# Self-attention in two-slot steps: order of transposes, outputs and small copies

## Chip, cores and metric

The kernel runs on one NeuronCore of a Trainium2 chip. The metric is the device time in microseconds of one execution, launch to end. The engines are named as in the profile: PE (TensorE, with PEld for its weight loads), DVE (VectorE), ACT (ScalarE), POOL (GpSimd) and SP (SyncE, which issues the transfers).

## What is computed

A decoder block on x (8 x 224 x 512, float32) with a context (8 x 750 x 384). Three layers follow one another, each with a residual sum and a layernorm behind it:

```
x = layernorm(x + self_attention(x))     # 16 heads of 64
x = layernorm(x + cross_attention(x, context))
x = layernorm(x + ffn(x))                # ternary weights, 8-bit activations

def self_attention(t):
    t = t * rsqrt(mean(t*t) + eps) * norm_w
    q, k, v = t @ Wq, t @ Wk, t @ Wv     # split into 16 heads
    q = q / |q| * (q_gamma + 1) * 8      # norm over each head's 64 numbers
    k = k / |k| * (k_gamma + 1) * 8
    s = tanh(q k^T / 50) * 50 / 8
    return softmax(s) v @ Wo
```

Only the self-attention is touched by the change.

## The kernel before

The 1792 rows of x lie in 14 tiles of 128 rows. Self-attention works on four groups `g` of two batch elements (448 columns). Inside a group it goes through eight pairs of heads `hp`, so the main loop has 32 slots, `m = 8 g + hp`. Two slots, an even and an odd one, belong together: in the even slot m the generator `project_pair` computes q and k of the slots m+2 and m+3 together, by a scheme with seven half-size products in place of eight (`mm_x`, `mz` as `mm_z`), and it is advanced piece by piece with `next(pair)` between other work. Instructions are issued on each compute engine in the order in which this Python code emits them (`manual_schedule`). Only the transfers on SP are ordered by a planner.

What a slot does, with names and lines of the kernel before:

- `self_scores(m)` (L490): PE makes the scores (`sc_a`, L500), ACT applies tanh (L510) and exp (L516) into `pr`.
- `inverse_sums(m)` (L520), a generator: DVE sums `pr` over blocks of 32 by a transposing reduction (L526, `sm_q`), three copies on ACT gather the partitions (L536), DVE adds and inverts (L539, L544, `sm_i`), three copies on ACT spread the result over partitions (L550), and DVE transposes it into `rc_a` (L558). It is advanced with `next(sums)`, in part in the following slot.
- `self_values(m - 1)` (L564): PE multiplies the previous slot's `pr` with the values (`ov_a`, L572), DVE scales into `oT` (L580). In groups 0 and 2 POOL copies 64 columns of `oT` into `oT_tail` (L585), since an output tile straddles two groups.
- `head_norms(m + 2, ...)` (L424), a generator used in even slots: DVE reduces the squares of q and k (L430, `nm_q`), four copies on ACT bring the neighbour quarter (L440, `nm_o`), and POOL adds, clamps and takes the power -1/2 for the two slots (L444, L445, L129 `nm_i`). This last part is emitted in the odd slot.
- `scale_qk(m)` (L455): DVE transposes `nm_i` (L458) and scales q and k with it (L463). The scores of slot m need this.
- `project_v` (L468): PE computes values of one tile (`mm_v`, L474), ACT copies them out (`copy_v`, L486).
- For the next group: `square` and `rms_norms` (ACT L245, DVE L249, POOL L129 `rms_rs`) when `hp == 0`, `scale_x` (ACT L256, `xn`) for one tile a slot, `transpose_xn` (PE L264, `tr_x`) and `copy_xn` (DVE L268, `xnT`) a slot later, for `hp` 1 to 3 or 4. `sum_input` (POOL L360 to L364) and `sum_weights` (POOL or DVE, L327 to L330) prepare operands of the seven products.
- `self_output` (L587): PE multiplies a finished tile of the previous group with Wo (`mm_o`, L600), DVE adds it to x (L609). The list `out_at` says in which `hp` of each group that happens. The tile is then put on `due`; in the next slot `layernorm` takes its statistics (DVE L136 to L138), its root on POOL (L129 `ln_rs`), and at the end of the slot DVE scales x (L152).

Some loops of the self-attention share PSUM buffers: `mm_x`, `mm_z`, `mm_v`, `tr_x` and `mm_o` take turns in three (`a_mm`).

Of the kernel before, what the change touches and what calls it, by code (L numbers as in the profile page):

```python
# [20 lines left out]
F32 = mybir.dt.float32  # L21
BF16 = mybir.dt.bfloat16
# [11 lines left out]
B, S, DIM = 8, 224, 512  # L34
# [4 lines left out]
P = 128  # L39
# [6 lines left out]
NPAIR = HEADS // 2  # L46
# [16 lines left out]
def decoder_block(ctx: ExitStack, tc: tile.TileContext, a: dict, out: bass.AP):  # L63
    nc = tc.nc
# [75 lines left out]
    def layernorm(tiles):  # L140


        n = len(tiles)
        mv = stat.tile([P, n, 2], F32, tag=f"ln_mv{n}", name="ln_mv")
        ve = stat.tile([P, n, 1], F32, tag=f"ln_ve{n}", name="ln_ve")
        rs = stat.tile([P, n, 1], F32, tag=f"ln_rs{n}", name="ln_rs")
        for j, i in enumerate(tiles):
            statistics(x[i], mv[:, j, :], ve[:, j, :])
        rsqrt(rs[:, :, 0], ve[:, :, 0])
        def scale():  # L150
            for j, i in enumerate(tiles):
                nc.vector.tensor_scalar(  # L152
                    x[i], x[i], mv[:, j, 0:1], rs[:, j, :], ALU.subtract, ALU.mult
                )

        return scale
# [54 lines left out]
    TAIL = G % P  # L211
# [5 lines left out]
    with tc.tile_pool(name="a_sb", bufs=2) as sb, tc.tile_pool(  # L217
        name="a_mm", bufs=3, space=PSUM
    ) as ps_mm, tc.tile_pool(name="a_sc", bufs=2, space=PSUM) as ps_sc, tc.tile_pool(
        name="a_ov", bufs=1, space=PSUM  # L220
# [20 lines left out]
            nc.gpsimd.memset(pr[KEYS[1][1] :, :, 1], 0.0)  # L241

        def square(i):
            sq = sb.tile([P, DIM], F32, name="sq_x", bufs=1)
            nc.scalar.activation(sq, x[i], AF.Square, accum_out=rms[:, i : i + 1])  # L245

        def rms_norms(i0, i1):
# [12 lines left out]
        def transpose_xn(i):  # L260
            y = xn.pop(i)
            trs[i] = tr = ps_mm.tile([P, KD, P], F32, tag="mm", name="tr_x")
            for k in range(KD):
                nc.tensor.transpose(tr[:, k, :], y[:, k * P : (k + 1) * P], ident)  # L264

        def copy_xn(i):
            c = i * P % (2 * G)
            nc.vector.tensor_tensor(  # L268
                xnT[:, :, c : c + P], trs.pop(i), norm_w.to_broadcast([P, KD, P]),
                ALU.mult,  # L270
            )
# [152 lines left out]
        def head_norms(m, i0, i1):  # L424

            quarter = sb.tile([P, 2, 4 * NB], F32, name="nm_q")[:, i0:i1]
            quarter = quarter.rearrange("p n b -> p (n b)")
            nc.vector.tensor_reduce(  # L430
                quarter,
                sq_pair[:, i0:i1].rearrange("p n u w (b c) -> p (n u w b) c", c=Q32),
                AX.X, ALU.add, apply_transpose=True,
            )
            yield
            other = sb.tile([P, 2, 4 * NB], F32, name="nm_o", bufs=1)[:, i0:i1]
            other = other.rearrange("p n b -> p (n b)")
            for q in range(P // Q32):
                o = q ^ 1
                nc.scalar.copy(  # L440
                    other[q * Q32 : (q + 1) * Q32], quarter[o * Q32 : (o + 1) * Q32]
                )
            yield
            nc.gpsimd.tensor_tensor(quarter, quarter, other, ALU.add)  # L444
            nc.gpsimd.tensor_scalar(quarter, quarter, 1e-24, None, ALU.max)  # L445
            for i in range(i0, i1):
                inv[m + i] = sb.tile([P, 2, 2 * NB, 1], F32, name="nm_i")
                at = (i - i0) * 4 * NB
                rsqrt(
                    inv[m + i].rearrange("p u b o -> p (u b o)"),  # L450
                    quarter[:, at : at + 4 * NB],
                )
            yield
# [66 lines left out]
        def inverse_sums(m):  # L520

            quarter = sb.tile([P, 2, 2, NB, NT, P // Q32], F32, name="sm_q", bufs=1)
            for u in range(2):
                nc.vector.tensor_reduce(  # L526
                    quarter[:, u, :, :, :, 0].rearrange("p j b t -> p j t b"),
                    prs[u].rearrange("p j t (b c) -> p j t b c", c=Q32),
                    AX.X, ALU.add, apply_transpose=True,
                )  # L530
            yield


            flat = quarter.rearrange("p u j b t g -> p (u j b t) g")
            for g in range(1, P // Q32):
                nc.scalar.copy(flat[:Q32, :, g], flat[g * Q32 : (g + 1) * Q32, :, 0])  # L536
            yield
            tot = sb.tile([Q32, 2, 2, NB], F32, name="sm_t", bufs=1)
            nc.vector.tensor_reduce(  # L539
                tot.rearrange("p u j b -> p (u j b)"),  # L540
                quarter[:Q32].rearrange("p u j b t g -> p (u j b) (t g)"), AX.X, ALU.add,
            )
            isum = sb.tile([P, 2, 2 * NB, 1], F32, name="sm_i", bufs=1)
            nc.vector.reciprocal(  # L544
                isum[:Q32, :, :, 0].rearrange("p j (u b) -> p j u b", u=2),
                tot.rearrange("p u j b -> p j u b"),
            )
            yield
            for g in range(1, P // Q32):
                nc.scalar.copy(  # L550
                    isum[g * Q32 : (g + 1) * Q32, g // 2, :, 0],
                    isum[:Q32, g // 2, :, 0],
                )
            yield
            rcs[m] = sb.tile([P, 2, S], F32, name="rc_a", bufs=1)
            for j in range(2):
                half = slice(j * DH, (j + 1) * DH)
                nc.vector.transpose(  # L558
                    rcs[m][half].rearrange("p u q -> p (u q)"),
                    isum[half, j].to_broadcast([DH, 2 * NB, Q32]),  # L560
                )
            yield

        def self_values(m):  # L564
            g, hp = divmod(m, NPAIR)
            ov = ps_ov.tile([P, 2, 256], F32, name="ov_a")
            for u in range(2):
                vt, pr = v[2 * g + u, hp // 4], prs[u]
                for kt, (_, n) in enumerate(KEYS):
                    for j in range(2):  # L570
                        h0, c = j * DH, (2 * hp + j) % 8 * DH
                        nc.tensor.matmul(  # L572
                            ov[h0 : h0 + DH, u, :S],
                            lhsT=vt[:n, kt, c : c + DH],
                            rhs=pr[:n, j, kt, :],
                            start=(kt == 0),
                            stop=(kt == NT - 1),
                        )
            oT[m] = sb.tile([P, 2, S], F32, name="oT", bufs=15)
            nc.vector.tensor_tensor(oT[m], ov[:, :, :S], rcs.pop(m), ALU.mult)  # L580
            if g % 2 == 0:

                if hp == 0:
                    tails[g] = sb.tile([P, NPAIR, TAIL], F32, name="oT_tail", bufs=1)
                nc.gpsimd.tensor_copy(tails[g][:, hp, :], oT[m][:, 1, S - TAIL :])  # L585

        def self_output(g, i, hp0=0, hp1=NPAIR):  # L587
# [24 lines left out]
        tails, outs, due, scales = {}, {}, [], []  # L612
# [35 lines left out]
        for i in opened[0][2:]:  # L648
            project_v(i, 0)()

        out_at = [(), (1, 3, 5), (1, 3, 5, 6), (5, 6, 7)]
        nothing = iter(lambda: None, 0)
        sums = norms = nothing
        for m in range(NS):
# [9 lines left out]
            if even:  # L664
                next(pair)
                next(sums)
                if m > 0:
                    scale_qk(m)
                next(pair)
                next(sums)  # L670
                next(pair)
                next(sums)
                next(pair)
            next(sums)
            if m > 0:
                self_values(m - 1)
            next(norms)
            next(pair)
            self_scores(m)
            for i in due:  # L680
                scales.append(layernorm([i]))
            due.clear()
            if even:
                scale_qk(m + 1)
            next(pair)
            if turned is not None:
                transpose_xn(turned)
                if not even:
                    copy_xn(turned)
            copy_v = lambda: None  # L690

            if hp % 4 < len(tiles):
                copy_v = project_v(tiles[hp % 4], c)
            if not even:
                copy_v()
            sums = inverse_sums(m)
            next(sums)
            norms = nothing
            if even:
                if pair is not nothing:  # L700
                    norms = head_norms(m + 2, 0, 2)
                next(norms)
                next(sums)
                copy_v()
                next(norms)
                next(sums)
                next(sums)
                if turned is not None:
                    copy_xn(turned)
            for f in scales:  # L710
                f()
            scales.clear()
# [700 lines left out]
```

## Time and profile before

| | us |
|---|---|
| median of 3 runs (lowest to highest) | 1728.12 (1725.98 to 1728.61) |
| the profiled execution | 1727.02 |
| its span, first to last instruction | 1725.2 |
| busy in the span: PE, PEld | 1671.9, 1148.8 |
| busy in the span: DVE, ACT, POOL | 1210.7, 938.7, 671.7 |

The page gives busy time per engine over the whole span. A row of the timeline has the start in us, the duration in us of the instructions merged into it, the engine, the line of the kernel, the operation with the tile written and the tiles read, and how many instructions there are; brackets hold the idle time of the engine before it and what ended that. A line of a windows table has the stretch, its length, the busy us (and instructions) of PE, PEld, DVE, ACT and POOL, the granted PE clock, the DMA share and the GB/s. A row of groups ends in busy us and mean ns of one, and the idle time before.

### The profile page before, as it was taken

The numbers are of one execution on the slowest core, as the hardware profiler recorded it, in microseconds if no ns is written. First come the engines' busy times: TensorE is split into PE (matmuls) and PEld (weight loads), VectorE is DVE, ScalarE is ACT, GpSimd is POOL, SyncE is SP. The second block draws the span as 40 slices with busy tenths as digits, with TensorE's granted clock in tenths as the row PEclk, the third lists the DMA queues.
The fourth block names the chain that finished last, engine by engine and source line by source line (L and its number), as shares of the span: only waits on it lengthen the run. The fifth ranks groups of instructions, "written<-read, shape, count | busy, mean of one in ns | idle before, by whom it ended". The sixth has DMA issues, their size and how long they took to land.

```text
span 1725.2 us, 24169 instructions
## 1 busy us (share of the span) xinstructions
PE 1671.9 (97%) x8962; PEld 1148.8 (67%) x8962; DVE 1210.7 (70%) x2402; ACT 938.7 (54%) x1752; POOL 671.7 (39%) x577
## 2 busy tenths in 40 slices
PE   8898999998999999999999999999999999999998
PEld 5666566566654777777676777777776776774443
DVE  3576566555773777677787787797875776886877
ACT  4677647555750566555565565464443543445663
POOL 3562342352430343444344244344343343443244
PEclk9999999999999999999999999999999999999999
DMA  7043112111312122111112112000000000031434
GB/s 256 25 137 126 43 55 74 43 51 48 123 64 90 63 74 101 50 50 64 43 48 84 44 50 82 22 34 34 1 3 29 4 5 24 1 129 40 74 81 106
DMA packets 85572, 106.71 MB, mean 62 GB/s; under 512 B 38352, under 2 KB 58832, under 8 KB 82512
## 3 DMA queue, kind: packets, MB, share of 16 engines
q1 hardware_dynamic: 85456, 105.19, 19.2%
q8 instruction: 70, 1.15, 0.3%
q14 instruction: 46, 0.38, 0.1%
HBM read 82.36 MB, written 14.16 MB: 56 GB/s over the span
## 4 chain that ended last, share of the span: by engine, by line
PE 87%; DVE 5%; ACT 3%; POOL 2%; issue 1%; DMA 1%; SPq 0%; POOLq 0%; DVEq 0%; ACTq 0%
PE mm_k L948 15%; PE mm_v L936 14%; PE sc_c L985 9%; PE ov_c L1079 9%; PE mm_co L194 6%; PE mm_q L961 6%; PE mm_f L1214 5%; PE mm_o L600 5%; PE mm_v L474 4%; PE mm_x L382 4%; PE mm_z L382 3%; PE dn L1302 2%; PE sc_a L500 2%; PE ov_a L572 2%; POOL nm_i L129 1%
## 5 line engine op out<-in xcount | busy, mean ns | idle before, releaser
L1069 POOL TENSOR_TENSOR csh<-cpT 125x672 f32<-125x672 f32 x128 | 207.3, 1620 | 579.7 <-DVE cpT L1059 553.5
L1067 ACT ACTIVATE cpT<-cpT 125x1344 f32<-125x1344 f32 x128 | 169.7, 1326 | 227.9 <-DVE cpT L1059 218.7
L948 PE MATMUL mm_k<-cT,xattn_Wk 128*128 128x375 f32 x768 | 259.4, 487 | 1.6 <-DMA cT<-ctxT 1.6
L936 PE MATMUL mm_v<-xattn_Wv,cT 128*125 128x256 f32 x1152 | 259.1, 379 | 0.0
L936 PEld LDWEIGHTS mm_v<-xattn_Wv,cT 128*125 128x125 f32 x1152 | 216.3, 188 | 28.8
L993 ACT COPY cpT<-sc_c 125x448 f32<-125x448 f32 x384 | 173.8, 560 | 108.2 <-PE sc_c L985 106.0
L948 PEld LDWEIGHTS mm_k<-cT,xattn_Wk 128*128 128x128 f32 x768 | 140.4, 189 | 102.1 <-issue 13.1
L1059 DVE TENSOR_TENSOR cpT<-cpT,mx_b 125x1344 f32<-125x1344 f32 x128 | 193.2, 1550 | 2.2
L995 DVE TENSOR_TENSOR cm<-sc_c,cpT 125x448 f32<-125x448 f32 x128 | 74.0, 619 | 147.4 <-ACT cpT L993 147.4
L985 PE MATMUL sc_c<-cqT,ckT 64*125 64x224 f32 x1536 | 163.5, 359 | 3.0 <-DVE cqT L969 3.0
L1079 PE MATMUL ov_c<-cpT,cv 125*64 125x224 f32 x1536 | 159.4, 357 | 0.0
L985 PEld LDWEIGHTS sc_c<-cqT,ckT 64*125 64x125 f32 x1536 | 140.8, 185 | 27.4 <-ACT ckT L955 14.3
L129 POOL TENSOR_TENSOR nm_i<-nm_q,mhalf 128x28 f32<-128x28 f32 x32 | 153.4, 4807 | 1.4
L1079 PEld LDWEIGHTS ov_c<-cpT,cv 125*64 125x64 f32 x1536 | 104.6, 137 | 47.3 <-issue 17.9
L955 ACT COPY ckT<-mm_k 128x375 f32<-128x375 f32 x128 | 59.2, 462 | 127.3 <-PE mm_k L948 127.3
L961 PEld LDWEIGHTS mm_q<-xT,xattn_Wq 128*128 128x128 f32 x512 | 96.8, 190 | 16.2
L474 PE MATMUL mm_v<-wv,xnT 128*128 128x512 f32 x224 | 107.5, 627 | 0.0
L961 PE MATMUL mm_q<-xT,xattn_Wq 128*128 128x224 f32 x512 | 107.2, 352 | 0.0
L600 PE MATMUL mm_o<-attn_Wo,oT 128*128 128x512 f32 (+1 forms) x224 | 100.0, 601 | 0.0
L1214 PE MATMUL mm_f<-ternary,xqT 128*128 128x512 bf16 x448 | 98.7, 379 | 0.9 <-DVE x L1106 0.9
L194 PE MATMUL mm_co<-xattn_Wo,coT 128*128 128x512 f32 (+1 forms) x256 | 98.1, 594 | 0.0
L1070 POOL TENSOR_TENSOR csm<-csh 125x224 f32<-125x224 f32 x128 | 93.8, 732 | 10.0
(187 smaller groups left out, 2643.5 us busy)
## 6 DMA issues: line engine op xcount, KB each, us to landing
w_pair<-w_sums_all SPq DMA_DIRECT2D x24, 512.0 KB, 4.1
cT<-ctxT SPq DMA_DIRECT2D x8, 1125.0 KB, 5.7
w_stage<-w_gateT SPq DMA_DIRECT2D x8, 1024.0 KB, 5.2
w_stage<-w_upT SPq DMA_DIRECT2D x8, 1024.0 KB, 5.1
w_stage<-w_downT SPq DMA_DIRECT2D x8, 1024.0 KB, 5.2
tern<-w_t SPq DMA_DIRECT2D x24, 256.0 KB, 2.3
ternary<-tern SPq DMA_DIRECT2D x3, 2048.0 KB, 12.6
w_pair<-attn_Wq SPq DMA_DIRECT2D x36, 128.0 KB, 2.2
```

Of the source, the lines that this page charges most:

```text
L194: nc.tensor.matmul(mm[row : row + m, :], lhsT=oT[:, k, at : at + m], rhs=w[:, k, :], start=(k == 0), stop=(k == NPAIR - 1),)
L474: nc.tensor.matmul(mm, lhsT=xnT[:, k, at : at + P], rhs=wv[:, k, c * 512 : (c + 1) * 512], start=(k == 0), stop=(k == KD - 1),)
L600: nc.tensor.matmul(mm[row : row + lhsT.shape[-1], :], lhsT=lhsT, rhs=wo[:, hp, :], start=(hp == 0), stop=(hp == NPAIR - 1),)
L936: nc.tensor.matmul(mm[:, i, :], lhsT=cT[:, k, c * CT : (c + 1) * CT], rhs=xwv[:, k, g * VN : (g + 1) * VN], start=(k == 0), stop=(k == KC ...
L948: nc.tensor.matmul(mm, lhsT=xwk[:, k, hp * P : (hp + 1) * P], rhs=cT[:, k, c * HALF : (c + 1) * HALF], start=(k == 0), stop=(k == KC - 1),)
L961: nc.tensor.matmul(mm, lhsT=xwq[:, k, hp * P : (hp + 1) * P], rhs=xT[:, k, :], start=(k == 0), stop=(k == KD - 1),)
L985: nc.tensor.matmul(sc[j][:, i, :], lhsT=kT[h0 : h0 + DH, ct * CT : (ct + 1) * CT], rhs=qT[h0 : h0 + DH, :], start=True, stop=True,)
L993: nc.scalar.copy(pT[:, j, 2 * c2 : 2 * c2 + 2, :], sc[j])
L1059: nc.vector.tensor_tensor(pT[:, j], pT[:, j], nm[:CT, j] .rearrange("p (o q) -> p o q", o=1) .to_broadcast([CT, NCT, S]), ALU.add,)
L1069: nc.gpsimd.tensor_tensor(half, pT[:, j, 0:3], pT[:, j, 3:6], ALU.add)
L1079: nc.tensor.matmul(ov[h0 : h0 + DH, :], lhsT=v[:, ct, hq * DH : (hq + 1) * DH], rhs=pT[:, j, ct, :], start=(ct == 0), stop=(ct == NCT - 1),)
L1214: nc.tensor.matmul(mm, lhsT=xqTs[i][:, k, :], rhs=w[:, k, cols], start=(k == 0), stop=(k == KD - 1),)
```

## The change

- In a slot that has both, the transposes `transpose_xn` are emitted behind the value projection instead of ahead of it; in odd slots `copy_v` comes before `copy_xn`.
- The statistics and the root of `layernorm` for the tiles on `due` are emitted right behind `self_values`, ahead of the norm roots, where they stood behind `self_scores`.
- In group 2 the output of `hp = 6` moves to `hp = 7`, so that all outputs but the last group's `hp = 6` lie in odd slots.
- `oT_tail` gets the pool's two buffers instead of one.
- The four copies of L440 and the three of L550 go from ACT to DVE. The three of L536 stay on ACT. In a pair of slots that is 10 of 16 small copies.
- The generators lose the yields around these copies: in a slot's second half the copies, the sums and the transposes into `rc_a` are emitted together, in the following slot.
- The squares that `square` writes and nobody reads become bfloat16.

```diff
         def square(i):
-            sq = sb.tile([P, DIM], F32, name="sq_x", bufs=1)
+            sq = sb.tile([P, DIM], BF16, name="sq_x", bufs=1)
...
                 AX.X, ALU.add, apply_transpose=True,
             )
-            yield
             other = sb.tile([P, 2, 4 * NB], F32, name="nm_o", bufs=1)[:, i0:i1]
             other = other.rearrange("p n b -> p (n b)")
             for q in range(P // Q32):
                 o = q ^ 1
-                nc.scalar.copy(
+                nc.vector.tensor_copy(
                     other[q * Q32 : (q + 1) * Q32], quarter[o * Q32 : (o + 1) * Q32]
                 )
             yield
...
-            yield
             for g in range(1, P // Q32):
-                nc.scalar.copy(
+                nc.vector.tensor_copy(
                     isum[g * Q32 : (g + 1) * Q32, g // 2, :, 0],
                     isum[:Q32, g // 2, :, 0],
                 )
-            yield
...
-                    tails[g] = sb.tile([P, NPAIR, TAIL], F32, name="oT_tail", bufs=1)
+                    tails[g] = sb.tile([P, NPAIR, TAIL], F32, name="oT_tail")
...
-        out_at = [(), (1, 3, 5), (1, 3, 5, 6), (5, 6, 7)]
+        out_at = [(), (1, 3, 5), (1, 3, 5, 7), (5, 6, 7)]
...
-                next(pair)
-                next(sums)
-                next(pair)
-                next(sums)
-                next(pair)
+                for _ in range(3):
+                    next(pair)
             next(sums)
             if m > 0:
                 self_values(m - 1)
+            for i in due:
+                scales.append(layernorm([i]))
+            due.clear()
             next(norms)
             next(pair)
             self_scores(m)
-            for i in due:
-                scales.append(layernorm([i]))
-            due.clear()
             if even:
                 scale_qk(m + 1)
             next(pair)
+            copy_v = lambda: None
+
+            if hp % 4 < len(tiles):
+                copy_v = project_v(tiles[hp % 4], c)
             if turned is not None:
                 transpose_xn(turned)
-                if not even:
-                    copy_xn(turned)
-            copy_v = lambda: None
-
-            if hp % 4 < len(tiles):
-                copy_v = project_v(tiles[hp % 4], c)
-            if not even:
-                copy_v()
-            sums = inverse_sums(m)
-            next(sums)
             norms = nothing
             if even:
+                sums = inverse_sums(m)
+                next(sums)
                 if pair is not nothing:
                     norms = head_norms(m + 2, 0, 2)
                 next(norms)
                 next(sums)
                 copy_v()
-                next(norms)
-                next(sums)
-                next(sums)
                 if turned is not None:
                     copy_xn(turned)
+            else:
+                copy_v()
+                if turned is not None:
+                    copy_xn(turned)
+                sums = inverse_sums(m)
+                next(sums)
```

More of the change, by code (lines that the diff above doesn't have):

```diff
@@ L685, in decoder_block @@
             next(pair)
-            if turned is not None:
-                transpose_xn(turned)
-                if not even:
-                    copy_xn(turned)
             copy_v = lambda: None
@@ L693, in decoder_block @@
                 copy_v = project_v(tiles[hp % 4], c)
-            if not even:
-                copy_v()
-            sums = inverse_sums(m)
-            next(sums)
+            if turned is not None:
+                transpose_xn(turned)
             norms = nothing
             if even:
+                sums = inverse_sums(m)
+                next(sums)
                 if pair is not nothing:
@@ L704, in decoder_block @@
                 copy_v()
-                next(norms)
-                next(sums)
-                next(sums)
                 if turned is not None:
                     copy_xn(turned)
+            else:
+                copy_v()
+                if turned is not None:
+                    copy_xn(turned)
+                sums = inverse_sums(m)
+                next(sums)
             for f in scales:
```

## Prediction

> **What bounds the kernel now.** I read the page first, then busy time by stage, the waits of TensorE (PE), and last the timeline around each of its waits.
>
> ```profile
> span 1725.2 us, 24169 instructions
> PE 1671.9 (97%) x8962; PEld 1148.8 (67%) x8962; DVE 1210.7 (70%) x2402; ACT 938.7 (54%) x1752; POOL 671.7 (39%) x577
> ```
>
> PE is busy for 97% of the span, so an edit that leaves the matmuls alone can win only PE's idle 53 us and whatever PE does slowly. The stages (columns: window, its length, then PE, PEld, DVE, ACT, POOL busy us, granted clock) say where that is:
>
> ```profile
> 0.00:40.00 40.00, 32.76 (x111) 19.84 (x112) 14.20 (x32) 16.74 (x36) 13.66 (x20) 1.00 0.78 276
> 40.00:548.00 508.00, 473.79 (x2347) 316.73 (x2346) 305.74 (x470) 296.12 (x730) 197.62 (x125) 0.97 0.20 67
> 548.00:1725.00 1177.00, 1165.34 (x6508) 812.25 (x6506) 890.72 (x1900) 625.83 (x987) 460.40 (x433) 1.00 0.17 52
> ```
>
> Self-attention runs from 40 to 548 us; there PE idles 34.2 us, and there alone the clock is below 1.00. Cross-attention and the feed-forward idle 11.7 us in 1177, so what the first stage saves should arrive at the end. The waits of PE in that stage (line waited for, total us, times, longest):
>
> ```profile
> PE tr_x L264 <- ACT xn L256: 16.4, 6, 4.7
> PE sc_a L500 <- DVE qk L463: 8.3, 4, 5.0
> PE mm_z L382 <- DVE qk L396: 4.8, 3, 2.4
> PE mm_x L382 <- ACT qk L400: 4.0, 4, 1.8
> PE mm_x L382 <- ACT qk L406: 0.6, 1, 0.6
> ```
>
> They sum to 34.1 us, all of that idle time. DVE, ACT and POOL are busy 60%, 58% and 39% of the stage: none is the bound; latency is. One transpose wait, in the timeline of slots 16 and 17:
>
> ```profile
> 295.93 0.97 ACT L440 COPY nm_o<-nm_q 32x56 f32<-32x56 f32 x4 [0.60 <-DVE nm_q L430]
> ...
> 296.92 0.62 ACT L550 COPY sm_i<-sm_i 32x14 f32<-32x14 f32 x3
> ...
> 300.96 0.72 ACT L256 ACTIVATE xn<-x,rms_rs 128x512 f32<-128x512 f32 x1 [1.16 <-POOL rms_rs L129]
> ...
> 301.74 1.11 PE L264 MATMUL tr_x<-ident,xn 128*128 128x128 f32 x4 [3.67 <-ACT xn L256]
> ...
> 302.64 5.76 PE L474 MATMUL mm_v<-wv,xnT 128*128 128x512 f32 x8
> ```
>
> ACT does seven small copies (1.6 us), then the squares, then `xn`; PE waits 3.67 us with value matmuls behind it that need nothing of this. Those eight then take 5.76 us, against 3.60 in slots without a wait, because the clock fell:
>
> ```profile
> 301.00:309.00 8.00, 7.26 (x16) 3.37 (x18) 3.66 (x5) 4.82 (x10) 0.00 (x0) 0.63 0.00 0
> ...
> 345.00:395.00 50.00, 50.00 (x239) 33.70 (x239) 30.08 (x50) 26.45 (x64) 24.70 (x15) 1.00 0.16 48
> ```
>
> The longest score wait is slot 24's:
>
> ```profile
> 412.83 9.57 POOL L129 TENSOR_TENSOR nm_i<-nm_q,mhalf 128x28 f32<-128x28 f32 x2
> ...
> 422.37 0.55 POOL L129 TENSOR_TENSOR ln_rs<-ln_ve,mhalf 128x1 f32<-128x1 f32 x1
> 422.95 0.55 DVE L152 TENSOR_SCALAR x<-x,ln_mv,ln_rs 128x512 f32<-128x512 f32 x1 [6.36 <-POOL ln_rs L129]
> ...
> 426.04 2.99 PE L500 MATMUL sc_a<-qk 64*128 64x224 f32 x16 [4.96 <-DVE qk L463]
> ```
>
> The layernorm root stands behind the two norm roots on POOL; DVE sits 6.36 us in L152 with slot 24's scaling of q and k behind it. And slot 17's norm roots start late, because the tail copy ahead of them needs a buffer that matmuls still read:
>
> ```profile
> 315.48 0.24 POOL L585 COPY oT_tail<-oT 128x64 f32<-128x64 f32 x1 [14.55 <-PE mm_o L600]
> ```
>
> [...] after gaps of 3.67 and 4.73 us the next 8 us have clock 0.63 and 0.58; after 1.44 us, 1.00. [...] after 2.18 us (at 497) ten us have 0.83. [...] L463 x2 takes 2.22 us beside POOL additions (at 108), but 1.28 inside a norm root (at 447). A copy inside a norm root is not shown. [...] ACT's copies take 200 ns for 14 columns and 235 for 56.
>
> **The change part by part.**
>
> *Transposes behind the values.* Same matmuls, reordered on PE in nine slots. The long waits are 3.67 (at 62.9), 4.73 (175.1) and 3.67 (301.7) = 12.1 us. Cover: 3.6 us of value matmuls, and `xn` earlier by the 1.6 us of copies that leave ACT, together 5.2, more than each. The cold clock after them costs 5.76 - 3.60, about 2.1 each, 6.3. The short ones (94.0, 211.9, 341.8) are 3 x 1.44 = 4.3; slot 11 at 211.9 has no values to hide behind, but the 1.6 us suffice. Sum 22.7. Late next: in slot 2 the first scores need POOL's roots. They ran at 77.37 with scaled q ready at 76.0; the POOL chain moves up only by 1.6, to 74.5, while PE would be there at 77.4 - 5.8 = 71.6: 2.9 given back. Behind the later transposes lie 6.9 us or more of output matmuls, which cover the same chain. Also queued: `copy_xn` on DVE comes 3.6 us later, with the odd slot's two L526 behind it; I count them done 7.4 us after the scores and the scaling 9.9 after, where PE needs it at 12.2. PSUM's three buffers turn in another order: mm_z of slots 2 and 4 waits for a value copy on ACT, done at about the time that PE gets there: 0.
>
> *Outputs in odd slots only.* Slot 22's output goes to slot 23. Its statistics and root then come in slot 24, with no norm roots in that slot. Slot 22's ov_a and tail copy come 6.9 us sooner, so the roots of slot 24 end at about 418 at the latest, before their scores. Gone: 4.96, 0.22 (mm_x at 415.9), and cold matmuls, 2.99 + 2.21 against 2 x 1.78 = 1.6. Sum 6.8.
>
> *Layernorm before norms.* With outputs in odd slots no slot has both roots; POOL's order differs in one place only (the tail copy before that ln_rs). 0 by itself.
>
> *Second `oT_tail` buffer.* Slot 17's roots start at about 302 instead of 315.7: the waits at 323.9 (0.34) and 331.3 (2.40) go: 2.7.
>
> *Copies to DVE.* 68 of L440 and 96 of L550 leave ACT: 68 x 0.235 + 96 x 0.200 = 35 us less. DVE's price is that of nearly equal copies in cross-attention:
>
> ```profile
> L1020 DVE COPY mx_s<-mx_r 32x28 f32<-32x28 f32 x252 | 45.8, 182 | 4.8
> L1042 DVE COPY mx_n<-mx_n 32x21 f32<-32x21 f32 x189 | 31.9, 169 | 3.8
> ```
>
> At 0.2 and 0.17: 30 us more on DVE, mostly beside matmuls (1.8 per pair of slots of some 31). For the gain: the softmax starts 1.6 us sooner after those copies, so the L400 waits shrink: 471.1 by 1.6, 279.6 by 0.27; at 149.4 the next scores wait for the roots, 0.8 left; slot 30 gets its q 0.6 sooner. Sum 3.3. For the loss: DVE's three copies take 0.5 where it idled 0.27 for ACT; 0.25 in three late slots, 0.7. The roots inside: bounds are 0 (as L463 at 447) and one root, 4.8 us per collision; I take 0.
>
> *bf16 squares, fewer yields, SP.* The squares are thrown away and keep their row's 0.63 us. SP has the same transfers; two loads of first weights swap places, each landing in some 2 to 4 us: 0.
>
> Sum: 22.7 - 2.9 + 6.8 + 2.7 + 3.3 - 0.7 = 31.9, less 2.0 (a choice) for waits that a faster PE uncovers: 29.9. The profiled execution took 1727.0 us (span 1725.2 and 1.8 around it): 1697.1. The median of the runs, 1728.1, is 1.1 above it: **1698**.
>
> **Rivals.** *Slower: DVE copies blocked behind norm roots.* Place: groups 1 and 3, where no tail copy delays the roots, so the sm_i copies come just as they start; and each even slot, where they run inside the second root. Price: a 4.8 us block less 0.5 of own time; some 1.7 us of slack before slot 28's scores leaves 2.6 in 8 pairs, and 1.0 in 15: 36. With the gain of 30: 1734. It decides from 2 us per pair (30/15). Against it: L463 at 447 runs inside a root undisturbed. [...]
>
> *Partly: the root chain takes over.* 9.6 us of POOL per pair are fixed; if each long wait gives back half, as slot 2's does: 22.7/2 + 6.8/2 + 2.7/2 = 16.1, +3.3 - 2.7: 16.7, so 1711. For it: nine waits of L458 for nm_i. Against it: 180 to 210 and 345 to 395 us, full pairs with no PE idle time.
>
> *Nothing arrives.* The end of the stage could be set by loads. Against it: the first context was issued at 483.7, long before 548; about 1728.
>
> **How the numbers follow.** The sum's case 0.68 (own range 1688 to 1708, up to all waits but a few gone), partly 0.15, nothing 0.05, blocked copies 0.12. Range 1688 to 1720. A measurement here tells about 0.2%, 3.5 us: faster 0.83, same 0.05, slower 0.12.
>
> **What would show it.** Right: tr_x gone from PE's waits, 40 to 548 shorter by about 30 with idle below 10 and clock near 1.00, no tail copy waiting for mm_o, nm_o and sm_i on DVE at 170 to 200 ns. Wrong: sm_i or nm_o copies of microseconds on DVE; sc_a or mm_z waits growing by what tr_x loses; more idle time after the stage.

## The result

| | before | after |
|---|---|---|
| median of 4 runs (lowest to highest), us | 1727.4 (1725.98 to 1728.61) | 1696.38 (1694.41 to 1697.73) |
| span of the profiled execution, us | 1725.2 | 1695.6 |
| ratio of the times, 95% interval | | 0.982 (0.9803 to 0.9837) |

The changed kernel is 31.0 us faster by the medians and 29.6 by the spans. The prediction was 1698, faster. In the changed kernel a line number of the self-attention is one to three lower than before: L473 makes the values, L499 the scores, L582 is the tail copy, L439 and L548 are the copies that moved.

From the page after, busy time:

```profile
PE 1664.2 (98%) x8962; PEld 1146.9 (68%) x8962; DVE 1241.4 (73%) x2566; ACT 906.3 (53%) x1588; POOL 672.4 (40%) x577
```

The same 8962 matmuls. PE's idle time, span less busy time, was 53.3 us and is 31.4: 21.9 less. Its busy time is 7.7 less. The matmuls are the same, so I put that down to the clock: over the span, the mean granted clock was 0.991 and is 0.996. The two parts make up the 29.6. DVE has 30.7 us more, ACT 32.4 less.

The stages after. The self-attention ends some 30 us sooner (the first transposes of cross-attention run at 519.2 instead of 548.4), so its window here is 40 to 517, two us short of its end:

```profile
40.00:517.00 477.00, 464.18 (x2343) 313.43 (x2343) 335.00 (x626) 265.34 (x574) 198.39 (x125) 0.99 0.22 71
517.00:1695.00 1178.00, 1167.32 (x6512) 813.66 (x6510) 890.63 (x1900) 626.16 (x987) 460.22 (x433) 1.00 0.17 52
```

In the stage PE idles 477.0 - 464.2 = 12.8 us (the same up to 519.2), where it was 34.2, and the clock is 0.99 instead of 0.97. Behind it nothing changed: 10.7 us idle in 1178, against 11.7 in 1177. What the first stage saved did arrive at the end. PE's waits in the stage, after:

```profile
PE sc_a L499 <- DVE qk L462: 5.6, 3, 2.0
PE mm_z L382 <- DVE qk L396: 5.3, 4, 1.6
PE mm_x L382 <- ACT qk L400: 0.7, 2, 0.4
...
PE mm_z L382 <- ACT v L485: 0.5, 1, 0.5
```

The row of tr_x (16.4 us, six times) is gone. The mm_x waits for L400 fell from 4.0 to 0.7, the score waits from 8.3 to 5.6. The waits of mm_z rose from 4.8 to 5.8, of which 0.5 is new in kind: it waits for a value copy.

A transpose in the timeline after, the one that waited 3.67 us at 301.7 before:

```profile
288.32 3.70 PE L473 MATMUL mm_v<-wv,xnT 128*128 128x512 f32 x8
...
289.09 0.72 ACT L256 ACTIVATE xn<-x,rms_rs 128x512 f32<-128x512 f32 x1 [1.17 <-POOL rms_rs L129]
...
291.86 0.60 PE L264 MATMUL tr_x<-ident,xn 128*128 128x128 f32 x4
```

`xn` ends at 289.8, while PE multiplies values until 291.9: 2.1 us of cover to spare. The eight value matmuls take 3.70 us, where they took 5.76 behind the wait.

Slot 24, whose scores waited 4.96 us before:

```profile
385.05 7.13 PE L597 MATMUL mm_o<-attn_Wo,oT 128*128 128x512 f32 x16
...
388.64 9.57 POOL L129 TENSOR_TENSOR nm_i<-nm_q,mhalf 128x28 f32<-128x28 f32 x2
...
400.03 1.78 PE L499 MATMUL sc_a<-qk 64*128 64x224 f32 x16
...
400.88 0.55 POOL L129 TENSOR_TENSOR ln_rs<-ln_ve,mhalf 128x1 f32<-128x1 f32 x1 [0.78 <-DVE ln_ve L138]
```

The output fills PE while the norm roots run, the scores start without a wait and take 1.78 us at a granted clock of 1.00, where they took 2.99 at 0.57, and the layernorm's root comes 2.7 us after the norm roots end. All sixteen tail copies wait for nothing but their own input or the engine's order; none waits for mm_o.

### The profile page after: what moved, and what is told of

It is laid out like the page before. It is cut to its first block, busy times and chain, and to the rows that moved or that the text cites. A ratio compares the mean times of both kernels' runs of the same rounds, so it can differ in the third digit from the quotient of the medians.

```text
span 1695.6 us, 24133 instructions
## 1 busy us (share of the span) xinstructions
PE 1664.2 (98%) x8962; PEld 1146.9 (68%) x8962; DVE 1241.4 (73%) x2566; ACT 906.3 (53%) x1588; POOL 672.4 (40%) x577
## 3 DMA queue, kind: packets, MB, share of 16 engines
q8 instruction: 70, 1.15, 0.3%
## 4 chain that ended last, share of the span: by engine, by line
PE 92%; DVE 4%; POOL 1%; issue 1%; DMA 1%; ACT 1%; POOLq 0%; SPq 0%; DVEq 0%
PE mm_k L941 15%; PE mm_v L929 14%; PE sc_c L978 9%; PE ov_c L1072 9%; PE mm_co L194 6%; PE mm_q L954 6%; PE mm_f L1207 5%; PE mm_o L597 5%; PE mm_v L473 5%; PE mm_x L382 5%; PE mm_z L382 4%; PE sc_a L499 3%; PE ov_a L569 3%; PE dn L1295 2%; PE mm_qk L291 1%
## 5 line engine op out<-in xcount | busy, mean ns | idle before, releaser
L941 PEld LDWEIGHTS mm_k<-cT,xattn_Wk 128*128 128x128 f32 x768 | 140.0, 189 | 101.1 <-issue 11.8
L473 PE MATMUL mm_v<-wv,xnT 128*128 128x512 f32 x224 | 101.4, 597 | 0.0
```

The lines of the kernel that those rows point to most:

```text
L473: nc.tensor.matmul(mm, lhsT=xnT[:, k, at : at + P], rhs=wv[:, k, c * 512 : (c + 1) * 512], start=(k == 0), stop=(k == KD - 1),)
L941: nc.tensor.matmul(mm, lhsT=xwk[:, k, hp * P : (hp + 1) * P], rhs=cT[:, k, c * HALF : (c + 1) * HALF], start=(k == 0), stop=(k == KC - 1),)
```

## Experiments

The runs were made in three groups, and the kernel before was timed again beside each: 1726.06, 1726.23 and 1726.4. The ratios and gains on the kernel before are against these. Line numbers in the kernels differ by a few.

**One edit alone, on the kernel before.**

*Transposes behind the values*

```diff
             next(pair)
-            if turned is not None:
-                transpose_xn(turned)
-                if not even:
-                    copy_xn(turned)
             copy_v = lambda: None
...
                 copy_v = project_v(tiles[hp % 4], c)
+            if turned is not None:
+                transpose_xn(turned)
             if not even:
                 copy_v()
+                if turned is not None:
+                    copy_xn(turned)
```

> The kernel before with one edit: the transposes behind the value projection, copy_v before copy_xn in odd slots. By the sum of the prediction: the long transpose waits 3.67, 4.73 and 3.67 shrink by the 3.6 us of value matmuls to 0.1, 1.1 and 0.1, the cold clock of 6.3 us after them goes, two of the three short waits go and the one of slot 11 (1.44), which has no values, stays; slot 2 gives back 4.4, since the root chain on POOL starts no sooner. Gain 15.6 us, so about 1712 of 1727.4. Rival, that the copies leaving ACT carry the gain: under 6 us, 1721 or more.

Measured 1712.29 (1711.69 to 1714.46), ratio 0.9917 (0.9902 to 0.9932): 13.8 us. The tr_x waits fell from 16.4 to 2.3 us in two places. Slot 2 gives part of it back, now in mm_x 2.22 (for POOL's L445), sc_a 0.66 and mm_z 2.33. The mm_x waits of 1.77 for ACT and the 4.96 of slot 24 stay, as they should.

*Copies to DVE, without the yields around them* (both copies and the loop of `next` as in the diff of the change)

```diff
-            yield
...
-                nc.scalar.copy(
+                nc.vector.tensor_copy(
```

> The kernel before with one edit: the nm_o and sm_i copies on DVE, with the yields around them removed. By the sum: xn comes 1.6 us sooner, so the long transpose waits shrink to 2.1, 3.1 and 2.1 (4.8 gained, and a part of the cold clock, 1), the short ones go (4.3), the L400 and score waits give 3.3, DVE costs 0.7: gain 12.7 us, about 1715. Rival, that the copies carry the whole change: gain 25 or more, 1702. Rival, that copies are blocked behind norm roots: slower than before.

Measured 1718.14 (1713.72 to 1721.8), ratio 0.9954 (0.9936 to 0.9971): 7.9 us, where 12.7 were expected. The six executions spread over 8 us, the longest with the lowest mean clock (0.991 at 1721.8, 0.995 at 1713.72), so this gain is known to 3 us only; the profile is of one of 1714.09. In it the transposes' waits fell further than by 1.6 each (3.67, 4.73 and 3.67 to 1.47, 3.08 and 1.47; the short ones gone), but slot 24's score wait grew from 4.96 to 6.16, and mm_z waits for L396 rose from 4.8 to 9.7 in sum. My reading, not tried by itself, is that a PE that arrives sooner meets the same root chain.

*Second `oT_tail` buffer, with the bf16 squares*

```diff
-            sq = sb.tile([P, DIM], F32, name="sq_x", bufs=1)
+            sq = sb.tile([P, DIM], BF16, name="sq_x", bufs=1)
...
-                    tails[g] = sb.tile([P, NPAIR, TAIL], F32, name="oT_tail", bufs=1)
+                    tails[g] = sb.tile([P, NPAIR, TAIL], F32, name="oT_tail")
```

> The kernel before with the second oT_tail buffer, and the bfloat16 squares, which free the memory for it[...]. By the sum: the tail copy no longer waits for mm_o, the score wait of 0.34 and the mm_z wait of 2.40 in slot 18 go: gain 2.7 us, about 1724.7. Rival, that slot 18 waits for something else: 0, 1727.4.

Measured 1722.94 (1720.63 to 1725.03), ratio 0.998 (0.9972 to 0.9988): 3.1 us. Slot 18's waits of 0.34 and 2.40 are gone. By the shapes the second buffer takes 8 x 64 x 4 bytes = 2 KB of a partition, and the smaller squares free 512 x 2 bytes = 1 KB. That the buffer needs this space was my reason for making the two edits together; no run has one without the other, so none shows it.

*Outputs in odd slots*

```diff
-        out_at = [(), (1, 3, 5), (1, 3, 5, 6), (5, 6, 7)]
+        out_at = [(), (1, 3, 5), (1, 3, 5, 7), (5, 6, 7)]
```

> The kernel before with one edit: group 2's last output at hp 7 instead of 6. By the sum: the score wait of 4.96 in slot 24 goes, with 0.22 before it and 1.6 of cold clock behind it: gain 6.8 us, about 1720.6. Rival, that the wait only moves to another slot: 2 us or less, 1725.4 or more.

Measured 1720.19 (1717.95 to 1722.24), ratio 0.9962 (0.9947 to 0.9976): 5.9 us, and the 4.96 is gone.

*Layernorm roots ahead of the norm roots*

```diff
-            next(norms)
-            next(pair)
-            self_scores(m)
             for i in due:
                 scales.append(layernorm([i]))
             due.clear()
+            next(norms)
+            next(pair)
+            self_scores(m)
```

> The kernel before with one edit: statistics and roots of layernorm ahead of the norm roots; the output of group 2 stays at hp 6. By the prediction's reading of slot 24 (a layernorm root queued behind two norm roots on POOL): the root runs at about 413 instead of 422, L152 no longer holds DVE, the scores wait 0.5 instead of 4.96: gain 6.0 us, about 1720, as much as moving the output. Rival, that the slot is late because of its 6.9 us of output matmuls, not because of the queue: 0.

Measured 1722.67 (1719.55 to 1724.58), ratio 0.9974 (0.9964 to 0.9983): 3.6 us. TensorE in the timeline of slot 24:

```profile
423.21 1.78 PE L500 MATMUL sc_a<-qk 64*128 64x224 f32 x16 [0.60 <-DVE qk L463]
...
429.52 1.78 PE L382 MATMUL mm_z<-xnT,w_pair 128*128 128x224 f32 x8 [1.30 <-DVE qk L396]
```

With the short root (at 414.37) ahead of the long ones (from 415.72) the scores wait 0.60 instead of 4.96, but the next mm_z now waits 1.30. So this edit alone cures most of what moving the output cures. They are two cures of one wait, and their gains should not add; the two were not run as a pair. The gains of the other four sum to 13.8 + 7.9 + 3.1 + 5.9 = 30.7, against 31.0 for the whole. That does not show that the four are independent: each gain is uncertain by 1 to 3 us, and the next run finds that the first two overlap.

**One edit undone, in the changed kernel.**

*Transposes back ahead of the values* (the first diff, reversed)

> The kernel after with the transposes back ahead of the values and copy_xn ahead of copy_v. By the sum: the long waits come back reduced by the copies' 1.6 us, to 2.1, 3.1 and 2.1, with some 3.6 of cold clock, less 2.0 that slot 2 waits now anyway: loss 8.9 us, about 1705. Rival, that the copies had covered them already: 1698 or less.

Measured 1704.76 (1700.89 to 1706.41), ratio 0.9873 (0.9853 to 0.9892). It loses 8.4 us against the changed kernel's 1696.38, less than the 13.8 that it wins alone, since the copies on DVE cover part of the same waits: tr_x waits of only 1.46, 3.08 and 1.46 come back, 6.0 of the 16.4.

*One tail buffer again*

```diff
-                    tails[g] = sb.tile([P, NPAIR, TAIL], F32, name="oT_tail")
+                    tails[g] = sb.tile([P, NPAIR, TAIL], F32, name="oT_tail", bufs=1)
```

> The kernel after with one oT_tail buffer. By the sum: slot 18 waits 0.3 and 2.4 again: loss 2.7 us, about 1699. Rival, that PE, which now comes to slot 18 sooner, waits longer than it did before: 6 or more, 1702.

Measured 1700.9 (1700.18 to 1702.08), ratio 0.9848 (0.9833 to 0.9863), a loss of 4.5 us, between the theory's 2.7 and the rival's 6. The waits of 0.34 and 2.73 in slot 18 are back; the second was 2.40 in the kernel before, so the rival's longer wait is no more than 0.33 us. The two intervals overlap, and the rest of the loss is within what they leave open.

*Copies back on ACT, at their new places in the order*

```diff
-                nc.vector.tensor_copy(
+                nc.scalar.copy(
```

> The kernel after with the seven copies back on ACT, without yields around them. By the sum: the L400 and score waits come back (3.3, less 0.7), slot 9's transposes wait 1.1, slot 11's 1.44, slot 2's roots come 1.6 later: loss 6.7 us, about 1703. Rival, that beside hidden transposes the copies are worth nothing: 1697.

Measured 1726.87 (1725.59 to 1728.97), ratio 1.0001 (0.9992 to 1.0009). That was a miss: the engine alone costs the whole gain. PE's largest waits in the stage:

```profile
PE mm_x L382 <- ACT qk L400: 14.3, 6, 3.8
```

and one of them, in the timeline:

```profile
147.90 0.98 ACT L439 COPY nm_o<-nm_q 32x56 f32<-32x56 f32 x4 [3.42 <-DVE nm_q L430]
...
149.83 2.34 ACT L485 COPY v<-mm_v 32x512 f32<-32x512 f32 x4
...
156.42 0.53 ACT L400 COPY qk<-mm_x 128x448 f32<-128x448 f32 x1
...
157.01 2.67 PE L382 MATMUL mm_x<-x_sums,w_pair 128*128 128x224 f32 x8 [3.75 <-ACT qk L400]
```

Without the yield the nm_o copies stand in ACT's order ahead of the sm_q copies and the value copies. They wait 3.42 us for DVE's L430 (15 such waits in the stage, 51.2 us in sum), and all of ACT waits with them, down to the eviction L400 for which PE then waits 3.75. On DVE the copies find their input ready at the same place (in the changed kernel DVE idles 1.1 us in all ahead of its 60 in the stage), since there they follow the instruction that they need on its own engine. Two readings were open: the copies are worth 30 us once the other edits are in, or the place is what cost it. The next run decides.

*Copies back on ACT, with the yields and places of the kernel before*

```diff
+            yield
...
-                nc.vector.tensor_copy(
+                nc.scalar.copy(
...
-                for _ in range(3):
-                    next(pair)
+                next(pair)
+                next(sums)
+                next(pair)
+                next(sums)
+                next(pair)
```

(and the other `next` lines of the change, reversed)

> The changed kernel with the nm_o and sm_i copies on ScalarE again, and this time also with the stops (the yields) and the places in the queue that the kernel before gave them. Theory (the single gains add, and what the run with the engine alone undone lost came from copies standing ahead of the value copies on ScalarE): the gains of the other edits alone were 13.8 for the transposes, 3.1 for the tail buffer and 5.9 for the output in odd slots, together 22.8 off 1726.2, so about 1703.5, 7 us above the changed kernel; no wait of mm_x for ScalarE longer than about 2 us. Rival (the copies' engine is worth 30 us as soon as the other edits are in, wherever the copies stand): 1725 to 1728, with 14 us of mm_x waiting for ScalarE as in that run.

Measured 1701.23 (1700.35 to 1703.3), ratio 0.9853 (0.984 to 0.9867), with the changed kernel timed again beside it:

> The changed kernel itself, unaltered, so that the other three stand beside it on the same chip. Both theories: a ratio of 0.982 to the kernel before, about 1696.

which took 1694.91 (1694.79 to 1698.11), ratio 0.9819 (0.9806 to 0.9833). So the copies' edit as a whole, engine and places, is worth 6.3 us in company and 7.9 alone, and the longest mm_x wait for ACT is 1.8. The rival is out: of the 30 us that the engine alone lost, about 24 were the place in ACT's order.

**Beyond the change: what is left.** Slots 2 and 8 still wait for the norm roots. The timeline of the changed kernel ahead of slot 2's scores:

```profile
65.13 0.73 POOL L330 TENSOR_TENSOR w_sums<-wk,w_sums 128x256 f32<-128x256 f32 x1
...
66.82 9.57 POOL L129 TENSOR_TENSOR nm_i<-nm_q,mhalf 128x28 f32<-128x28 f32 x2
```

From 60.08 on eight weight sums of a later pair, this the last, stand ahead of the roots that the scores need, which then wait 1.97 us at 74.21. The next run makes the sums of pair 2 before the loop, and takes the tail copy out of `self_values` (as `copy_tail`) to put it behind the norm roots:

```diff
+        sum_weights(2, nc.gpsimd)

         out_at = [(), (1, 3, 5), (1, 3, 5, 7), (5, 6, 7)]
...
             next(norms)
+            if m > 0:
+                copy_tail(m - 1)
             next(pair)
             self_scores(m)
...
-            if g == 0 and hp in (0, 2, 4):
+            if g == 0 and hp in (2, 4):
                 sum_weights((2, 3, 0)[hp // 2], nc.gpsimd)
```

> The changed kernel with two pieces of GpSimd's queue moved: the tail copy comes behind the norm roots of the next slot, not ahead of them, and the weight sums of pair 2 are made in the lead-in, not in slot 0. Theory (what is left of waits in slots 2 and 8 is the chain through the norm roots, and GpSimd's order sets it): the scores' waits of 1.97 at 74.21, 1.80 at 155.00 and 1.83 at 467.76 shrink or go, with some 1.5 us each of half-speed matmuls behind them, and with them a part of the mm_z waits (5.3 together): 7 to 9 us less than the changed kernel, about 1688. Rival (VectorE's order is the limit, since scale_qk stands behind other work there): only the scores' waits themselves go, 4 us less, about 1692, or the wait moves to mm_z and nothing is gained, 1696.

Measured 1685.54 (1684.61 to 1685.87), ratio 0.976 (0.9746 to 0.9773): 9.4 us faster than the changed kernel beside it, and PE's waits in the stage are

```profile
PE sc_a L499 <- DVE qk L462: 1.8, 1, 1.8
PE mm_x L382 <- ACT qk L400: 0.7, 2, 0.4
PE mm_x L382 <- ACT qk L406: 0.6, 1, 0.6
PE mm_z L382 <- ACT v L485: 0.5, 1, 0.5
```

The mm_z waits for L396 went altogether: they were DVE standing in the scaling L462, and that in POOL's roots, one chain and not two. What the weight sums and the tail copy each won was not tried apart. What the expectation had wrong is slot 28, whose 1.81 stays: POOL has been idle 11.8 us there before the norm's addition, and it is DVE that brings the copies late (L525, 2.10 us, and then L430, 2.00, stand ahead of them). There the rival's reason, DVE's order, holds.

The last run takes the addition L396 ahead of the scaling as well:

```diff
             add(m + 1, 1)
+            yield
...
             self_scores(m)
+            next(pair)
             if even:
                 scale_qk(m + 1)
```

> The same as the run with GpSimd's two pieces moved, and on VectorE the eviction-and-add of the next pair's mm_z (line 396) ahead of scale_qk instead of behind it. Theory (the mm_z waits for line 396, 5.3 us in 4 places, are VectorE's order): they go, so up to 5 us less than that run and about 1685. Rival (scale_qk later makes the scores later, which wait for it on the same engine): the scores' waits grow by what mm_z saves, so no less than that run or some 2 us more.

Measured 1684.17 (1683.17 to 1684.36), ratio 0.9751 (0.9738 to 0.9765). The interval overlaps that of the run before, and the waits are the same four: nothing was left for it to win. It is the fastest of all, but its lead of 1.4 us is below what a measurement here tells.

## Why the prediction was right, step by step

- *What bounds the kernel.* Right: PE's idle time in the self-attention fell by 21.4 us and the rest of the gain is its clock; the stages behind it added no idle time. One of its signs failed: idle time in the stage was to be below 10 us and is 12.8.
- *Transposes.* The six waits went, and the slow value matmuls with them (before, the eight at 302.64 took 5.76 us at a granted clock of 0.62; after, the eight at 288.32 take 3.70 at 1.00). The low clock was worth more than the 6.3 foreseen, since it had stretched the three late transposes too (1.11 us for 0.66). The give-back in slot 2 was foreseen as 2.9. The score wait is 1.97, with slow matmuls behind it (2.30 and 2.90 us for batches of 1.78) and a wait of 1.03 for L396 that was 1.12 before: 1.97 + 0.52 + 1.12 + 1.03 - 1.12 = 3.5 us. Right in mechanism. The single edits won less than their own expectations, 13.8 for 15.6 and 7.9 for 12.7; the two were not measured as a pair.
- *The PSUM wait of mm_z in slots 2 and 4, taken as 0.* Mis-sized: 0.53 us at 65.56 for the value copy, once, in slot 2.
- *Outputs in odd slots.* 6.8 foreseen, 5.9 measured alone.
- *Layernorm ahead of the norms.* "0 by itself" was meant beside the moved output. On the kernel before it wins 3.6. What it is worth in the changed kernel, with the output moved, was not tried.
- *Second tail buffer.* 2.7 foreseen; 3.1 alone, 4.5 when undone.
- *bf16 squares, 0.* Their duration is the same (0.63 us), as foreseen. The step left out my reason for them, the space of the second buffer, which no run tried.
- *Fewer yields, 0.* The whole came out with it, but no run has the copies on DVE with the yields left in. The step treated the engine and the place as separate edits; with the copies left on ACT the same places cost about 24 us.
- *Copies' price on DVE.* 30 us foreseen from the rows of cross-attention, 30.7 measured. Of the 164, most take 0.17 to 0.18 us.
- *Allowance of 2.0 for waits uncovered.* Mis-sized. New waits of mm_z at 109.2 and 135.8 are of this kind, 1.39 and 1.27, and slot 8 waits 1.80 and 1.64 where it waited 0.85 and 1.30. With the 0.53 of slot 2 that is 4.5 us, more than twice the allowance.
- *Own sum.* 29.9 foreseen, 29.6 by the spans, 31.0 by the medians. That it is so close is partly luck, since the terms above missed by some us both ways. The split agrees too, 7.9 of clock foreseen (6.3 + 1.6) and 7.7 found, and that is luck as well: a second profiled execution of the changed kernel has PE busy 1659.8 instead of 1664.2, so the clock's share is uncertain by 4 us.

*The rivals.* "Copies blocked behind norm roots" fell. The witness that the prediction called against it, L463, is no copy; the copies themselves show it now. The views of DVE and of POOL after:

```profile
75.35 0.54 DVE L548 COPY sm_i<-sm_i 32x14 f32<-32x14 f32 x3
...
115.65 1.58 DVE L439 COPY nm_o<-nm_q 32x56 f32<-32x56 f32 x4
```

```profile
115.46 1.14 POOL L364 TENSOR_TENSOR x_sums<-xnT,x_sums 128x448 f32<-128x448 f32 x1
```

The three copies at 75.35 run inside the roots at 66.82, shown above, at their own pace, and so do all fourteen groups of L548 in the stage that meet a norm root (0.54 to 0.56 us). The four at 115.65 begin during an addition of POOL and take twice their 0.77. Such a block shows three times in the stage, 0.5 to 1.0 us each. "The root chain takes over" was right in kind and too large. The six waits that the run with GpSimd's order moved removes sum to 9.1 us in the changed kernel, and at the same places it was 3.3 in the kernel before. So the chain took back about 5.8 us, an estimate from these waits, against 4.9 in the sum (2.9 and the allowance of 2.0) and half of all that was won in the rival. "Nothing arrives" fell with the stages' idle times.

## What to carry to other kernels

When an engine is busy for 97% of the span, list its waits of the one stage that has them, and ask of each what work that needs nothing could stand in front of it, and which short instruction stands behind a long one on the engine that it waits for. Moving a small operation is an edit of two things, its engine and its place in that engine's order: a copy right behind its producer found its input ready on the producer's engine here, and on another it held up all that stood behind it. Undo edits as well as making them alone: the transposes won 13.8 us alone and lost 8.4 when undone, so part of what they cure another edit cures too, and a sum of single gains that fits (30.7 of 31.0 here) does not show the parts to be independent. The waits that are left tell where to go next, here GpSimd's order, worth another 9.4 us.

## What the runs showed of the hardware

Short gaps of PE (1.8 to 2.0 us) were followed by slow matmuls in one execution and not in another. TensorE in slot 2, in the two profiled executions of the changed kernel:

```profile
74.21 2.30 PE L499 MATMUL sc_a<-qk 64*128 64x224 f32 x16 [1.97 <-DVE qk L462]
76.44 2.90 PE L382 MATMUL mm_z<-x_sums,w_sums 128*128 128x224 f32 x8
...
81.89 1.78 PE L382 MATMUL mm_z<-xnT,w_sums 128*128 128x224 f32 x8 [1.03 <-DVE qk L396]
```

```profile
73.39 1.78 PE L499 MATMUL sc_a<-qk 64*128 64x224 f32 x16 [1.96 <-DVE qk L462]
75.11 1.78 PE L382 MATMUL mm_z<-x_sums,w_sums 128*128 128x224 f32 x8
...
81.06 1.78 PE L382 MATMUL mm_z<-xnT,w_sums 128*128 128x224 f32 x8 [2.66 <-DVE qk L396]
```

Behind the same gap, 1.97 and 1.96 us, the two batches took 0.5 and 1.1 us longer in the one, at a granted clock of 0.76 (74.2 to 76.4 us) and 0.61 (76.4 to 79.4), and their usual 1.78 in the other. Here that cost nothing in the end: the next wait, which DVE sets, is shorter by as much (1.03 for 2.66), and from the scores to the batch behind that wait it is 7.68 us in the one and 7.67 in the other. At 467.8 it did cost: behind a gap of 1.83 the scores took 3.29 instead of 1.78, at a clock of 0.52, with output matmuls behind them and no wait to take it up, and the second execution has 1.78 behind its 1.81. In slot 8, at 155.00, the scores behind a gap of 1.80 took 1.78 in both. So the price of these gaps is a range, 0 to about 1.6 us.

DVE's copies ran longer beside some additions of GpSimd (of 0.73 to 1.15 us) and not beside its norm roots. In three places of the stage one copy that began during an addition ran on to about that addition's end: it took 0.62 us at 60.22, 0.99 at 115.65 (the first of the four in 1.58 us) and 1.02 at 232.44, for 0.17 to 0.18. The three copies of a group that met a root of 4.8 us took 0.54 to 0.56 us together, in all fourteen such groups.
